# An output product by seven, a new order of the period, and tables for the opening and the closing of a two-layer graph kernel

## The chip, the cores and the metric

The kernel runs on 1 core of one Trainium2 chip. The metric is the device time of one execution in microseconds (us), lower is better. Before the change three runs gave a median of 3567.93 us (3567.24 to 3570.02).

## The reference

64 graphs of 256 nodes with 512 features, all in fp32, and for each graph an adjacency mask. Two layers follow each other, each with a layer norm and a ReLU ahead of it and a residual behind it. Cut to what matters:

```
h = maximum(layernorm(x), 0)                        # layer 0
m = h @ map_w.T + map_b                             # 512 -> 512, 8 heads of 64
cos = normalized(m) @ normalized(m).T  per head;  cos_adj = cos > 0.1
p = softmax(q @ k.T / 8, masked) * keep;  q, k = m @ q_w.T, m @ k_w.T
sem = (h @ gcn_map_w.T + gcn_map_b);  a = cos_adj * p
x = x + relu((a @ sem) @ gcn_W.T / (a.sum(-1) + 1))
h = maximum(layernorm(x), 0)                        # layer 1
q, k, v = h @ Wq, h @ Wk, h @ Wv                    # 512 -> 256, 4 heads of 64
out = softmax(masked(q @ k.T / 8)) @ v
x = x + out @ Wo + bo                               # 256 -> 512, the "output product"
```

## The kernel before, in words

All of the work is in fast_path (L153 to L1073 of the file); a general path behind a check at the end is not taken with this data. The graphs go through a software pipeline. A **period** `i` (L734) holds the steps of five graphs in different stages: the attention of layer 0 of graph `i` (`g`), the projections of layer 0 of graph `i+1` (`nx`), the norm and transposition of graph `i+2` (`n2`), the norm, projections and attention of layer 1 of graph `i-1` (`b`), and the output product and store of graph `i-2` (`bb`). A step is a function of a few instructions under a short name; the list ORDER (L716) says in which order a period calls them, and since the kernel is written with a manual schedule, that is the order of the instructions on every engine. An engine works through its own instructions strictly in that order and waits on semaphores for what comes from elsewhere. SyncE (SP) issues nearly all transfers, also in order.

The names that matter below:
- `sc0` to `sc3`: scores of layer 0 (L474, 64 rows of the array); `ex`: their exp on ScalarE (ACT); `mk`: mask on VectorE (DVE); `hv`: the two halves of a row summed on GpSimd (POOL); `co`: cosines (L511, 64 rows); `fo`, `fb`: the threshold on DVE; `fa`, `fz`: more halves on POOL; `av`: values (L501, 64 columns); `sm`, `pn`, `zb`: sums (32 columns).
- `m`, `s`, `q`, `k`, `j`, `v` with 1 to 7 and a to g: products in the manner of Strassen and Winograd (class Seven, L296). A product of 2x2 blocks takes seven block products (steps 1 to 7 on TensorE, PE) into two PSUM regions u and z, and steps a to g bring them out: a, b, c and g on ACT or DVE with the bias, d, e, f as sums on DVE (L341). Step 4 writes where step 3 wrote, so it waits for b; 5 waits for d, 6 for e, 7 for f. The sums of blocks of the weights are made once by finish_seven (L82), four DVE subtractions, and those of the data per graph by left_factor (L277), four POOL operations (`lm`, `lh`, `lb`).
- `po0`, `po1` (product_out, L697): the output product of layer 1, for each half of the nodes two matmuls of 512 columns; `oa` (added, L703) adds it to x on DVE, `st` stores.
- `rt`, `rc`, `rk`: the sums are transposed on PE, inverted on DVE, and multiplied by keep on DVE; `ho`, `ha`: the heads are scaled and added to x on DVE; `nb`: statistics of layer 1's norm on DVE; `pb`: its power on POOL; `xb`, `fl`, `tr`, `jb`: scaling, splitting into 16-bit halves, transposing by DMA, joining; `un`: the unit vectors for the cosines, on DVE; `dv` (L694): the attention of layer 1 times its inverse sums, on DVE.

PSUM is a ring of 8 banks with which all products are served. SBUF buffers of one use share a tag; the tags "xn" (2 buffers) and "d" (6), "rn" (1) and "sms" (1) matter here.

Opening (L1001 to L1068): loads, 14 warming matmuls, then the layer 0 projections of graph 0 in straight order, with finish_seven in blocks of four subtractions between the products; then 63 periods, ORDER with those steps that have a graph; then closing (L878), which runs the attention of graph 63, layer 1 of graph 62 and then layer 1 of graph 63 in straight order. The chain of layer 1's norm in it (moments, powers, scaled, split, turn, join1) has nothing of another graph beside it.

Of the kernel before, what the change touches and what calls it, by code (L numbers as in the profile page):

```python
# [20 lines left out]
LN_EPS = 1e-5  # L21
# [8 lines left out]
class Weights:  # L30
# [30 lines left out]
    def load_w(self, key, name):  # L61
        ap = self.a[key]
        t = self.const.tile([128, ap.shape[0] // 128, ap.shape[1]], F32, name=name)
        self.nc.sync.dma_start(out=t, in_=ap.rearrange("(c p) f -> p c f", p=128))
        return t

# [15 lines left out]
    def finish_seven(self, t):  # L82
        sub = self.nc.vector.tensor_sub
        sub(t[:, 5], t[:, 2], t[:, 3])
        sub(t[:, 3], t[:, 3], t[:, 0])
        sub(t[:, 4], t[:, 2], t[:, 3])
        sub(t[:, 6], t[:, 1], t[:, 4])
# [14 lines left out]
    def load_rest(self):  # L102
        self.wv1 = self.load_seven("Wv", "wv1")
        self.wqk1 = self.load_seven(("Wq", "Wk"), "wqk1")
        self.wo1 = self.load_w("Wo", "wo1")
# [17 lines left out]
    def fold(self, gws, gt, bank, put, cs):  # L123

        nc, P = self.nc, 128
        NKC = self.gb.shape[1]
        for c in cs:
            p = bank(f"p_wc{c}", [P, NKC * P])
            for k in range(NKC):
                nc.tensor.matmul(p[:, k * P:(k + 1) * P], gws[k // 2][:, k % 2, c * P:(c + 1) * P], gt,  # L130
                                 start=True, stop=True)
            put(c, p)
# [4 lines left out]
    def fold_bias(self, gbb, gt, bank):  # L137
# [5 lines left out]
        nc.scalar.copy(self.bc, p)  # L143

    def put_seven(self, c, p):
        i, k = divmod(c, self.wc.shape[2])
        half = self.wc.shape[3]
        for j in range(2):
            self.nc.scalar.copy(self.wc[:, self.BLOCKS.index((i, j)), k, :], p[:, j * half:(j + 1) * half])


@with_exitstack
def fast_path(ctx, tc, a, w, chk, out):  # L153
# [28 lines left out]
    class Graph:  # L182
        pass

    graphs = {}

    def load(i):
        g = graphs.setdefault(i, Graph())
        g.i, g.e, g.d, g.far = i, {}, {}, {}
# [4 lines left out]
        return g  # L194


    def moments(g, tag):
        st = small.tile([P, NT, 6], F32, tag="st", name=f"st{tag}", bufs=2)
        g.mv = small.tile([P, NT, 2], F32, tag="mv", name=f"mv{tag}")
        for t in range(NT):  # L200
            nc.vector.bn_stats(st[:, t, :], g.xs[:, t, :])  # L201
            nc.vector.bn_aggr(g.mv[:, t, :], st[:, t, :])  # L202
        g.rs = small.tile([P, NT], F32, tag="rs", name=f"rs{tag}")
        nc.vector.tensor_scalar_add(g.rs, g.mv[:, :, 1], LN_EPS)
# [4 lines left out]
    def normalized(g, tag):  # L209
        g.xn = []  # L210
        for t in range(NT):
# [1166 lines left out]
```

## Time and profile before

| what | us |
|---|---|
| median of 3 runs | 3567.93 |
| the profiled execution | 3568.4 |
| its span on the core | 3566.6 |
| PE busy | 3523.6 |
| DVE, ACT, POOL busy | 2285.5, 2224.8, 2499.7 |
| one period (rt of one to rt of the next) | 54.55 |
| PE busy in the first 89.00 us, in the last 97.00 us | 73.20, 69.97 |

The page gives busy time for each engine, then the span in 40 slices of 89 us (a digit is the busy share in tenths), then the chain of work that ended last. A line of a group or of the timeline has the line of the code, the engine, the operation, and `out<-in` by tile names; PEld is the weight load, which runs beside the matmuls. On PE each fp32 matmul of the program shows as two records. Durations of matmuls overlap, so what one costs is read from one start to the next. In the timeline a bracket at the end of a line is the idle time ahead of it and what ended it.

### The profile page before, as it was taken

The page shows a single profiled execution, that of the slowest core. Times are in us where ns is not written, and L with a number is a line of the kernel's source. Part 1 is how long each engine was busy: PE and PEld are TensorE (multiplying, and loading weights), DVE is VectorE, ACT ScalarE, POOL GpSimd, SP SyncE. Part 2 cuts the span into 40 slices and gives each one's busy share as a digit, 9 for nine tenths or more (in the row PEclk, how much of TensorE's full clock was granted, in tenths as well). Part 3 has the DMA queues.
Part 4 walks back from the last instruction along what each step waited for, and adds up shares of the span by engine and source line. Part 5 has one row for each costly group of instructions (what it writes and reads, how often), then busy time and mean ns, then how long its engine had stood idle before and what let it go on. Part 6 is the DMA issues. An engine that isn't in the chain of part 4 may idle for free.

```text
span 3566.6 us, 77423 instructions
## 1 busy us (share of the span) xinstructions
PE 3523.6 (99%) x28983; PEld 2996.0 (84%) x28983; DVE 2285.5 (64%) x4718; ACT 2224.8 (62%) x5302; POOL 2499.7 (70%) x2612
## 2 busy tenths in 40 slices
PE   8999999999999999999999999999999999999997
PEld 7888888888888888888888888888888888888885
DVE  5666666656667666666566666666666766666654
ACT  3666666666666666666666666666666666666652
POOL 4777777677677777776776777777767777777662
PEclk9999999999999999999999999999999999999998
DMA  4333333323333333333333333333333333333321
GB/s 115 73 67 71 83 68 71 76 66 78 69 72 80 67 71 83 67 71 75 68 77 69 72 81 67 71 79 68 73 73 71 77 68 71 82 68 71 76 55 37
DMA packets 650851, 258.32 MB, mean 72 GB/s; under 512 B 562508, under 2 KB 616808, under 8 KB 650472
## 3 DMA queue, kind: packets, MB, share of 16 engines
q1 hardware_dynamic: 649736, 252.75, 31.8%
q8 instruction: 231, 3.78, 0.5%
q14 instruction: 148, 1.21, 0.1%
q10 hardware_dynamic: 544, 0.52, 0.0%
q0 software_dynamic: 192, 0.04, 0.0%
HBM read 94.41 MB, written 34.34 MB: 36 GB/s over the span
## 4 chain that ended last, share of the span: by engine, by line
PE 97%; DMA 1%; DVE 1%; ACT 1%; POOL 0%; issue 0%; SPq 0%; DVEq 0%; POOLq 0%; ACTq 0%
PE av L501 10%; PE p_m_z L316 7%; PE p_q_z L316 7%; PE sc L474 7%; PE p_qk_z L316 6%; PE p_k_z L316 6%; PE p_o L700 6%; PE p_s_z L311 6%; PE co L511 5%; PE p_s_u L311 5%; PE p_qk_u L316 5%; PE p_k_u L316 5%; PE p_q_u L316 5%; PE p_m_u L316 5%; PE sd L474 3%; PE p_v_z L311 3%
## 5 line engine op out<-in xcount | busy, mean ns | idle before, releaser
L542 POOL TENSOR_TENSOR d<-d,e 128x512 f32<-128x512 f32 x504 | 652.9, 1316 | 158.1 <-DVE e L547 136.4
L494 POOL TENSOR_TENSOR d<-e 128x512 f32<-128x512 f32 x376 | 470.7, 1273 | 345.6 <-DVE e L488 176.7
L481 ACT ACTIVATE e<-sc 128x512 f32<-128x512 f32 x520 | 268.3, 603 | 143.8 <-PE sc L474 143.8
L488 DVE SCALAR_TENSOR_TENSOR e<-mask,e 128x1024 f32<-128x1024 bf16 x128 | 157.6, 1232 | 300.5 <-ACT e L481 237.8
L490 DVE TENSOR_TENSOR e<-e,mask 128x1024 f32<-128x1024 f32 x256 | 307.4, 1221 | 2.7 <-ACT e L481 0.4
L527 DVE SCALAR_TENSOR_TENSOR e<-co,e 128x256 f32<-128x256 f32 (+1 forms) x1024 | 286.8, 346 | 19.8 <-ACT up L520 17.8
L251 POOL COPY flat<-xn 128x512 uint16<-128x512 uint16 x252 | 218.5, 906 | 86.9 <-ACT xn L243 86.9
L474 PE MATMUL sc<-qT,kT 64*128 64x256 f32 x2048 | 238.4, 383 | 0.5 <-ACT qT L334 0.5
L501 PE MATMUL av<-e,sem 128*64 128x256 f32 x2048 | 235.4, 382 | 2.1 <-DVE e L547 2.1
L334 ACT ACTIVATE u3p_m<-p_m_u,bm 128x128 f32<-128x128 f32 x128 | 40.0, 363 | 307.8 <-PE p_m_u L316 307.8
L700 PE MATMUL p_o<-wo,own 128*128 128x512 f32 x512 | 230.6, 593 | 0.0
L474 PEld LDWEIGHTS sc<-qT,kT 64*128 64x128 f32 x2048 | 192.8, 187 | 41.4 <-issue 20.9
L229 POOL TENSOR_SCALAR shift<-mv 128x2 f32<-128x2 f32 x125 | 27.8, 222 | 282.3 <-DVE mv L202 282.3
L501 PEld LDWEIGHTS av<-e,sem 128*64 128x64 f32 x2048 | 141.4, 137 | 93.0 <-ACT v L328 25.5
L201 DVE BATCH_NORM_STATS2 st<-xs 128x6 f32<-128x512 f32 x256 | 173.3, 677 | 50.5 <-DMA xs<-in_x_dram 47.0
L243 ACT ACTIVATE xn<-xs,shift,rs 128x512 f32<-128x512 f32 x250 | 197.8, 824 | 8.5 <-POOL shift L233 8.5
L511 PE MATMUL co<-nT 64*128 64x256 f32 (+1 forms) x2048 | 202.8, 337 | 0.0
L481 ACT ACTIVATE e<-sd 128x512 f32<-128x512 f32 x248 | 134.7, 595 | 106.7 <-PE av L501 78.1
L511 PEld LDWEIGHTS co<-nT 64*128 64x128 f32 x2048 | 166.9, 187 | 40.6 <-ACT up L520 20.9
L341 DVE TENSOR_TENSOR qT<-p_q_z,u2p_q 128x256 f32<-128x256 f32 x64 | 27.1, 424 | 255.0 <-PE p_q_z L316 255.0
L442 POOL TENSOR_TENSOR lengths<-lengths,root 128x16 f32<-128x16 f32 x64 | 186.4, 2912 | 3.8 <-DMA lengths<-rn 3.8
L576 ACT COPY sem<-heads 128x512 uint16<-128x512 uint16 x252 | 178.4, 777 | 6.4 <-DMA heads<-avs 5.9
(254 smaller groups left out, 9858.0 us busy)
## 6 DMA issues: line engine op xcount, KB each, us to landing
xs<-in_x_dram SPq DMA_DIRECT2D x64, 512.0 KB, 4.1
nT<-by_rn SPq DMA_DIRECT2D x128, 256.0 KB
out_dram<-xs SPq DMA_DIRECT2D x63, 512.0 KB, 3.1
own<-by_rz SPq DMA_DIRECT2D x126, 128.0 KB, 3.1
turn<-flat SPq DMA_TRANSPOSE x500, 2.5
ad<-in_adj_dram SPq DMA_DIRECT2D x64, 64.0 KB
far<-up SPq DMA_TRANSPOSE x256, 3.1
heads<-avs SPq DMA_TRANSPOSE x252, 2.5
```

The costliest lines, as they stand in the source:

```text
L251: copy(getattr(g, what)[:, t, k, :], g.xn[t].bitcast(U16).rearrange("p (d k) -> p k d", k=2)[:, k, :])
L311: nc.tensor.matmul(region, src[:, c, :], self.wt[:, block, c, :], start=p not in self.opened, stop=True, skip_group_check=True)
L316: nc.tensor.matmul(region[:, f, :], self.wt[:, block, c, f * P:(f + 1) * P], src[:, c, :], start=p not in self.opened, stop=True, skip_gro ...
L474: nc.tensor.matmul(ps[s][:, j, :], rows[h, c, j * P:(j + 1) * P], cols[h, c, :], start=True, stop=True)
L481: nc.scalar.activation(e[:, s, :], p.rearrange("p j q -> p (j q)"), AF.Exp, scale=SCALE)
L490: nc.vector.tensor_mul(e, e, m)
L494: nc.gpsimd.tensor_add(d, e[:, :, :S], e[:, :, S:])
L501: nc.tensor.matmul(av[s * DH:(s + 1) * DH, n, :], vs[:, j, (h0 + s) * DH:(h0 + s + 1) * DH], q[:, s, j * S:(j + 1) * S], start=(j == 0), s ...
L511: nc.tensor.matmul(ps[s][:, j, j * P:], g.nT[h, c, j * P:(j + 1) * P], g.nT[h, c, j * P:], start=(j == 0), stop=True, skip_group_check=True)
L527: nc.vector.scalar_tensor_tensor(e, p.rearrange("p j q -> p (j q)")[:, lo:hi], THRESHOLD, e, op0=ALU.is_gt, op1=ALU.mult)
L542: nc.gpsimd.tensor_add(g.d[c][:, :, q], g.d[c][:, :, q], g.e[c][:, :, lo:hi])
L700: nc.tensor.matmul(p, b.avs1[:, c, t * P:(t + 1) * P], w.wo1[:, c, :], start=(c == 0), stop=(c == NIC - 1))
```

## The change

Three things. First, the output product is one of the sevens: Wo is loaded in four blocks, its block sums are made in the opening (`fw0` to `fw3`), its data's block sums are four POOL steps `lw0` to `lw3`, written where the inverse sums `z` lay, and the steps are `w1` to `w7` and `wa` to `wg` with x in the place of a bias, on DVE (`onto`). Each product is one matmul of 256 columns. For the last graph by_halves does the same with five matmuls per half of the nodes and no block sums of the data. Second, ORDER is new; it serves periods 2 to 61. Third, periods 0 and 1 with all of the opening are one table (HEAD), and periods 62, 63 and 64 with all of the closing are another (TAIL); finish_seven is cut into single steps. Layer 1 of graph 62 then takes the steps of the period (`hy`, `zb` on halves). Besides: "xn" and "d" become one tag "xd" with 7 buffers, "rn" and "sms" one tag "row" with 1, and graph 3 is loaded early in HEAD rather than after period 0.

```diff
-        self.wo1 = self.load_w("Wo", "wo1")
+        self.wo1 = self.load_seven("Wo", "wo1")
...
-    def finish_seven(self, t):
...
+    def finish_one(self, t, n):
+        to, x, y = ((5, 2, 3), (3, 3, 0), (4, 2, 3), (6, 1, 4))[n]
+        self.nc.vector.tensor_sub(t[:, to], t[:, x], t[:, y])
...
+def by_halves(nc, p, rows, wt):
+
+    half = wt.shape[3]
+    for f, terms in enumerate((((0, 0), (1, 1)), ((0, 3), (0, 0), (1, 2)))):
+        for n, (c, block) in enumerate(terms):
+            nc.tensor.matmul(p[:, f * half:(f + 1) * half], rows(c), wt[:, block, 0, :],
+                             start=(n == 0 and f == 0), stop=(n == len(terms) - 1), skip_group_check=True)
...
-            setattr(g, f"left_{kind}", sb1.tile([P, 4, HC, P], F32, tag=tag, name=f"{tag}_{kind}{g.i}"))
+            setattr(g, f"left_{kind}", g.z.rearrange("p c (n q) -> p (c n) q", q=P)[:, :, None, :] if kind == "avs1"
+                    else sb1.tile([P, 4, HC, P], F32, tag=tag, name=f"{tag}_{kind}{g.i}"))
...
-            for c in range(HC):
+            for c in range(self.wt.shape[2]):
...
-        def biased(self, t, region, features):
-            if self.bias is None:
+        def biased(self, t, region, tokens, features):
+            if self.onto:
+                nc.vector.tensor_add(t, region, self.quarter(tokens, features))
+            elif self.bias is None:
...
-    def product_out(b, t):
-        p = bank(f"p_o{b.i}_{t}", [P, D])
-        for c in range(NIC):
-            nc.tensor.matmul(p, b.avs1[:, c, t * P:(t + 1) * P], w.wo1[:, c, :], start=(c == 0), stop=(c == NIC - 1))
-        return p
...
+    def outputs(b):
+        return Seven((b, "avs1"), w.wo1, None, lambda: b.xs, f"p_o{b.i}", tokens_first=True, onto=True)
 
-    ORDER = """
-        s2 s1 sc2 rk sc0 sc1 ho0 ho1 ha0 ha1 mt nb ex2 ex0 mk2 sc3
-        s3 sb m1 ex3 dv ex1 mk3 sa m2 sd m3 po0 po1 s5 pb xb0
-        xb1 ma un oa0 md mb fl01 mk1 m5 m4 mc co0 up0 co1 fl00 fl10
-        mk0 fl11 hv0 hv1 up1 oa1 tr00 tr01 tr10 jb0 st tr11 ft0 rq s4 me
-        fo0 sc ft1 se ld co3 co2 m6 s6 fo1 mf m7 k1 rr jb1 hv3
-        hv2 fa1 v1 mg fo2 fa0 fo3 lm0 up2 na lm1 ft2 lb0 lb1 lb3 pa
-        lm3 j2 j1 q1 j3 k3 q3 up3 va ja sf jd jb fb1 lb2 j4
-        jc fb0 j5 je xa0 v2 pl00 ft3 v3 vb xa1 vd k2 j6 pl10 v5
-        v4 jf qa fa2 fb2 fa3 fz2 fz1 bo1 ka pl11 kd vc ve fb3 kb
-        pl01 ta00 s7 j7 v6 ta01 ta10 k4 vf v7 kc jg sq0 sq1 k5 sd0
-        sg fz3 sd1 pn ey0 my0 fz0 hy0 ln av0 vg ey1 ja0 hs00 my1 av1
-        hy1 hs10 ay sm zb ls bo0 hs01 qb q2 ta11 ht00 ht01 ht10 ke to
-        hs11 hj00 ht11 qd iy ed q4 qc lm2 q5 qe rt k6 q6 kf li
-        ja1 lh2 lh0 lh1 lh3 k7 sy sp qf rc hj01 hj10 hj11 q7 zq kg
-        qg oy
-    """.split()
+    ORDER = """
+        sc3 rk ho0 sc0 ex3 sc1 ex1 ha0 rq ho1 ha1 dv lw0 sc2 w1 w3
+        w2 s1 lw1 lw3 nb wa wd ex2 s2 wb w4 w5 m1 mk2 pb xb0
+        lw2 xb1 fl00 fl11 fl01 ex0 wc we m2 w6 m3 sa un ma mb wf
+        sd w7 wg rr s3 md sb mk1 co2 co3 up3 up2 s4 hv2 mk3 mk0
+        fo2 fl10 m4 tr00 mc tr01 s5 tr10 st tr11 m5 sc se co0 co1 s6
+        jb0 hv3 hv0 hv1 ft2 me up0 m6 fo0 jb1 j1 fo3 mf fa0 lb2 lb0
+        lb1 v1 m7 lb3 up1 ld sf mg j2 v2 j3 v3 s7 lm0 na pa
+        vb ja mt xa0 jd fo1 ft0 fb0 va fa2 fa1 fz0 lm1 fa3 fb2 pl00
+        q1 fz2 pl01 ft1 ta01 ft3 fb1 fz1 bo1 q3 j5 v4 jb xa1 vc pl11
+        vd j4 jc je q2 v5 ve qa j6 jf v6 k1 ta00 ka vf sg
+        v7 pl10 ta11 ta10 j7 k3 jg lm3 bo0 sq1 sq0 qb vg sd1 sd0 fb3
+        ey0 av0 av1 ey1 ja0 q4 hs00 k2 hs01 kb k4 ja1 qd my0 my1 kc
+        pn hs10 ln hy0 hy1 zb fz3 lm2 sm lh2 ay ht00 ht01 ls hj00 hs11
+        lh0 lh1 ht10 hj01 qc kd hj10 iy q5 qe k5 ke ht11 lh3 to sy
+        q6 qf hj11 k6 li sp rt kf rc q7 qg oy ed k7 kg zq
+    """.split()
...
-            each(T, "po%d")(lambda t: bb.po.update({t: product_out(bb, t)}))
-            each(T, "oa%d")(lambda t: added(bb, t, bb.po[t]))
+            left("lw", bb, "avs1")
+            seven("w", outputs(bb))
...
+    HEAD = """
+        o.na00 o.na01 o.nr0 o.w0 o.ed0 o.dn0 o.xn00 o.tp00 o.tq00 o.xn01 o.tp01 o.tq01 o.lh00 o.lh01 o.lh03 o.fm0
+        o.fm1 o.l3 o.fm2 o.fm3 o.lh02 o.ed1 o.gb o.fp2 o.m1 o.fp0 o.m3 o.fp3 o.ma o.m2 o.mb o.fo2
+        o.m4 o.fq0 o.md o.fk0 o.mc o.m5 o.me o.fp1 o.m6 o.fo3 1.na o.mt0 o.mf o.q2 o.q1 o.m7
+        o.fk1 o.fo0 o.k1 o.fk2 o.sq1 o.fq1 o.fo1 o.mg o.sq0 o.na10 o.na11 o.nr1 o.ka o.lm0 o.bp o.pn
+        o.s1 o.q3 o.lm1 o.k2 o.bo o.lm2 o.qa o.fs0 o.fq2 o.ln 0.na o.fs1 o.qd o.lm3 o.k3 o.qb
+        o.s2 o.q4 o.q5 o.kb o.dn1 o.qc o.sa 0.pa o.fs2 o.qe o.xn10 o.sd 0.mt 0.xa0 0.pl01 0.xa1
+        o.s3 o.q6 o.k4 o.kc o.kd o.qf o.sb o.xn11 o.k5 o.fk3 o.s4 o.s5 o.ke o.sc o.se o.k6
+        o.s6 0.pl00 o.ls o.fw0 o.fw1 o.kf 0.sc2 0.ex2 o.k7 o.fs3 o.sf o.fj0 o.fq3 0.mk2 o.s7 o.tp10
...
+        1.co2 1.mk1 1.lw0 1.w3 1.tr11 1.ft3 1.up2 1.ft2 1.up0 1.ft0 1.mk3 1.w2 c.se1 c.se3 1.wb 1.fo2
+        1.lw1 1.wd 1.fo3 1.fb3 1.co1 1.jb0 1.jb1 1.up1 1.lw3 1.w4 1.bo1 1.lb0 1.w5 1.j1 1.ft1 1.j3
+        1.rq 1.fb2 1.fb0 1.lb1 1.lb3 1.lw2 1.fo1 1.fb1 1.wc 1.we 1.av1 1.av0 c.sm0 c.sm2 c.sm1 c.vs0
+        1.jb c.vs1 c.fi c.sm3 c.to c.hb0 c.hb1 1.rt 1.rc 1.w6 1.wf 1.j2 1.ja c.rk c.hm0 c.hp0
+        1.w7 1.jd 1.j4 1.lb2 1.j5 1.v2 1.v1 1.jc 1.je 1.j6 c.hm1 1.va 1.vd c.hp1 1.jf c.nb0
+        c.nb1 1.v3 1.vb 1.j7 1.v5 1.v4 1.jg c.nr c.dn 1.vc 1.sd0 1.ve 1.ey0 1.sd1 1.v6 c.xn0
+        c.xn1 c.tp1 c.tp0 1.ey1 c.tq0 1.vf 1.my0 1.my1 1.v7 1.vg 1.ay c.tq1 0.j1 0.ja 1.hy0 1.hy1
+        0.lb0 1.zb 0.v2 0.j3 0.j2 0.lb1 c.rq 1.zq 1.iy 0.lb3 0.lb2 1.wg 0.jb 0.jd 0.j4 0.j5
+        0.v1 0.v3 0.jc 0.je 1.oy 0.vb 0.va 0.rr 0.j6 0.v4 0.vc 0.vd 0.v5 0.jf 0.j7 0.ve
+        1.sy 0.dv 0.jg 0.v6 0.sd0 0.vf 0.sd1 1.bo0 0.w1 0.lw0 0.lw1 0.bo1 0.w3 0.ey0 0.my0 0.w2
+        2.st 1.st 0.lw3 0.lw2 0.bo0 0.ey1 0.my1 0.v7 0.vg 0.wb 0.wa 0.wd c.zl 0.ay 0.w5 c.zi0
+        c.zm0 c.zi1 0.w4 c.zm1 c.zk c.po0 0.wc 0.we 0.w6 0.wf c.po1 c.oa0 c.oa1 0.w7 c.wu 0.wg
+        c.st0 c.st1 0.st
+    """.split()
...
-        for i in range(B - 1):
-            period(i)
-        closing()
+        tables = {"o": opening_steps()}
+        heads, tails = {0: 0, 1: 1}, {2: B - 2, 1: B - 1, 0: B}
+        for n, i in heads.items():
+            tables[f"{n}"] = steps_of(i)
+        for name in HEAD:
+            table, name = name.split(".")
+            tables[table][name]()
+        for i in range(2, B - 2):
+            steps = steps_of(i)
+            for name in ORDER:
+                steps[name]()
+        tables = {"c": closing_steps()}
+        for n, i in tails.items():
+            tables[f"{n}"] = steps_of(i)
+        for name in TAIL:
+            table, name = name.split(".")
+            tables[table][name]()
```

opening_steps and closing_steps (new) hold the former steps of the opening and the closing under names of their own ("o." and "c." in the tables), cut smaller: for example `o.tp00` the four transposes of one half of the nodes, `c.zi0` the reciprocal of one half. steps_of is the former period, without the loop over ORDER.

## The prediction

> **What bounds the kernel now.** I read the page first (busy shares, slices, chain), then the stretches, then the PE timeline of one period in the middle and of both ends.
>
> ```profile
> span 3566.6 us, 77423 instructions
> ...
> PE 3523.6 (99%) x28983; PEld 2996.0 (84%) x28983; DVE 2285.5 (64%) x4718; ACT 2224.8 (62%) x5302; POOL 2499.7 (70%) x2612
> ...
> PE   8999999999999999999999999999999999999997
> ...
> PE 97%; DMA 1%; DVE 1%; ACT 1%; POOL 0%; issue 0%; SPq 0%; DVEq 0%; POOLq 0%; ACTq 0%
> ```
>
> TensorE is the bound: 97% of the chain, and only the first and the last slice are not full. So every us must come out of three things: PE's own work, waits in the first and last 90 us, and waits that a new order may put into the middle. The stretches say the same:
>
> ```profile
> 0.00:89.00 89.00, 73.20 (x544) 63.97 (x548) 50.95 (x111) 33.04 (x84) 44.27 (x53) 0.98 0.42 115
> ...
> 1780.00:1834.50 54.50, 54.50 (x452) 46.40 (x451) 35.26 (x73) 35.05 (x84) 39.28 (x42) 1.00 0.32 74
> ...
> 3470.00:3567.00 97.00, 69.97 (x543) 52.77 (x543) 46.18 (x90) 31.93 (x81) 21.14 (x23) 0.90 0.14 39
> ```
>
> Columns: stretch, length, busy us of PE, weight load, DVE, ACT, POOL, then granted clock. The middle one is a period (54.55 us from one rt product, 1781.64, to the next, 1836.19): PE busy throughout, the others with 15 to 19 us to spare.
>
> The price of PE work comes from the timeline (start, duration, what):
>
> ```profile
> 1786.29 1.03 PE L311 MATMUL p_s_u<-wc,hT 128*128 128x256 f32 x4
> 1787.25 3.72 PE L474 MATMUL sc<-qT,kT 64*128 64x256 f32 x32
> ...
> 1794.55 3.60 PE L700 MATMUL p_o<-wo,own 128*128 128x512 f32 x8
> 1797.99 1.03 PE L311 MATMUL p_s_z<-wc,sh_hT 128*128 128x256 f32 x4
> 1798.85 1.05 PE L316 MATMUL p_m_z<-sh_hT,wm 128*128 128x128 f32 x8
> ...
> 3498.77 2.08 PE L316 MATMUL p_qk_u<-h1T,wqk 128*128 128x128 f32 x8 [14.29 <-ACT h1T L267]
> ```
>
> Durations overlap, so the cost is start to start. Each fp32 matmul of the program is two records. Eight records 512 wide take 1797.99 - 1794.55 = 3.44 us (0.430 each); four 256 wide take 0.86 (0.215 each). A change of tile shape costs extra: the four of p_s_u ahead of the 64-row sc take 0.96. Over all neighbouring pairs that extra is 0.093 us, and nothing else in the middle exceeds the bare price: no idle over 0.06 us between 110 and 3476 us. The last line is the end's largest wait, 14.29 us, with the restart at half clock (2.08 against 1.06).
>
> **The change part by part**, against the profiled execution (3568.4 us; span 3566.6).
>
> *Output product by seven.* Before: 8 records of 0.430 per graph, 3.44 us. Now seven block products of one 256-wide matmul each: 14 records of 0.215, the price of the row with the same form (p_s_z), 3.01 us. Gain 0.43 for 63 graphs; the last graph's (by_halves) takes 10 matmuls for 8 equivalents, 0.86 more. 63 x 0.43 - 0.86 = -26.2 us; at the mean intervals of all pairs (0.429, 0.216) it is -24.8, which I take. The weight load of each (0.19 us) stays under the matmul, as in p_s.
>
> *More changes of tile shape.* The new ORDER puts q4, k2, k4 between the value products (av0, av1) and pn: one more change per period; the two end tables add the rest. Counting along PE's instruction order of both programs: 709 before, 784 after. The Trainium skill speaks against this: TensorEngine Tiling (Array Packing), Key Properties, says that changing the mode drains the engine. It gives no figure there; TensorE: Matmul & The Clock Gate, Step-by-step, puts a drain at about 128 cycles, 53 ns at 2.4 GHz. By that, 75 x 0.053 = 4.0 us; by the trace's 0.093, 7.0 us. The trace is taken: +7.0.
>
> *DVE and POOL work of the product.* DVE adds five more operations of 128x256 (7 against 2 of 128x512): 7 x 0.42 - 2 x 0.69 = +1.6 us per period on 35.3. POOL adds four lw sums of 128x128; no row has that size: 0.73 us (128x256) is the upper bound, half of it the lower; I take 0.45, as 128x512 costs 1.27 and 128x256 0.73. +1.8 on 39.3. Both stay far below 54, so in total they cost nothing; what matters is where they stand.
>
> *New waits at the period's start.* This is the unknown term. PE now comes from rt through q7, k7 and four sc to w1: 0.22 + 1.79 + 3.65 + 0.09 = about 5.76 us after rt starts. w1 needs dv. On DVE, in order ahead of dv: kf, rc, rk, ho0, ha0, ho1, ha1. Their rows:
>
> ```profile
> 1784.18 0.25 DVE L608 RECIPROCAL r<-rt 128x16 f32<-128x16 f32 x1
> 1784.47 0.86 DVE L618 TENSOR_SCALAR rk<-r,keep 128x8 f32<-128x8 f32 x2
> 1785.30 1.96 DVE L630 SCALAR_TENSOR_TENSOR o<-sem,rk 128x256 f32<-128x256 f32 x4
> 1787.18 1.28 DVE L636 TENSOR_TENSOR xs<-xs,o 128x512 f32<-128x512 f32 x2
> 1788.49 0.69 DVE L201 BATCH_NORM_STATS2 st<-xs 128x6 f32<-128x512 f32 x1
> ...
> 1790.44 1.23 DVE L490 TENSOR_TENSOR e<-e,mask 128x1024 f32<-128x1024 f32 x1
> ```
>
> k6 ends when rt starts; its result is there 0.2 later. Then kf 0.38, rc 0.29, rk 0.83, ho 1.88, ha 1.31, dv 0.65: dv ends 5.5 to 5.6, against 5.76. Just in time. w3, 0.43 after w1, needs dv and then lw0 (0.45 plus two handovers): late by up to 0.1. DVE goes on without a gap: nb 1.95, wa, wd, wb 1.1 (w4 waits for wb: on time to 0.1 late), mk2 1.2, wc, we, sa 1.2, un 1.4, wf 0.4. That ends 12.9 after rt; w7, which waits for wf, is due at 12.8. Behind w1, w3, w4, w7 stands all of PE's queue (s1, m1, m3, s3, co), so such a lateness is paid in full, once per period, as the chain hangs on rt again. Below nothing is excluded: PE had no idle there to give back. From above: 0.4 us, if each handover costs 0.05 more. I take 0.1, close to the sum: 60 x 0.1 = +6 us, and keep 0 and 24. Elsewhere I find cover of 0.2 us or more (s6 waits for se, j1 for jb1, sm for the last fz). On SP the output store now waits for wg, before the last turn; wg ends about 1 us before SP gets there (fl10 comes later on POOL). The shared buffers cost nothing in the middle: sms waits until the lengths' transfer has read its row, about 1.5 us earlier.
>
> *Opening.* PE idles 16.3 us up to 115 us (brackets of the PE timeline, summed), 2.8 of it before anything can run:
>
> ```profile
> 21.61 2.08 PE L316 MATMUL p_m_z<-sh_hT,wm 128*128 128x128 f32 x8 [3.15 <-DVE mT L341]
> ...
> 39.52 1.16 PE L316 MATMUL p_q_z<-sm_mT,wq 128*128 128x128 f32 x8 [2.67 <-DVE qT L341]
> ...
> 81.47 1.13 PE L316 MATMUL p_k_u<-sm_mT,wk 128*128 128x128 f32 x8 [3.41 <-ACT u5p_k L334]
> ```
>
> The 3.15 stands behind the four subtractions for wq on DVE; in the table they come later and one by one, and fold, q, k or s products stand between an m product and its successor. The start itself (statistics, pow, transposes, first product at about 10 us) is unchanged. I leave 5 us: -11.3, between -6 and -13.5. PE also ran at half clock from 21.6 to 25.0 after that wait: -1.7.
>
> *Closing.* PE idles 19.9 us from 3470 on, of which 14.3 in one wait (moments, pow, copies, turns and joins of graph 62 with nothing beside them). In the table periods 62 and 63 and the closing interleave, so that chain lies under other products. What remains is the last graph's own chain (values, sums, norm, transposes, scores, exp, reciprocals), with graph 62's j, v and w as fillers: I leave 7, so -12.9 (between -7 and -17), and -2.2 for the half clock after 3498.8. On the other side the last store is now 512 KB issued after wg, where it was 256 KB: its row lands in 3.1 us against 1.7: +2. The kernel's last 5.4 us (the check and what follows) stay.
>
> Sum: -24.8 + 7.0 + 6 - 11.3 - 1.7 - 12.9 - 2.2 + 2 = -37.9; 3568.4 - 37.9 = 3530.5. The median of the runs is 0.5 under the profiled one: 3530.
>
> **The rivals.**
> 1. *The new order's waits take the middle's gain.* At 0.5 us per period: 24 us more, 3554. For it: DVE has no gap for 12 us there, and four PE waits hang on it. Against: the sum ends within 0.1 us. Chance 0.17.
> 2. *Nothing waits.* The middle fits, and both ends keep only what no order can remove (about 3 us at each): -6 - 2 - 4 - 2 = 3516. For it: the old order has no wait in the middle either. Chance 0.13.
> 3. *Slower: DVE and POOL collide at the period's start.* The Trainium skill, SBUF — State Buffer, Who interferes with whom, says that a DVE instruction with two SBUF inputs and a GpSimd instruction that reads SBUF exclude each other for a whole instruction. The trace has such spread: the far products (L547, two SBUF inputs) take 0.41 to 0.97 us for one shape, the pow (L207) 0.73 to 1.76. The change puts lw0, lw1, lw3, lw2 beside dv, mk2, un, all with two SBUF inputs. By the rows alone the chain is 0.1 late; if each of three pairs blocks for 0.4 to 0.5 us, it is 1.4 late: 60 x 1.3 = 78 more, 3608. It decides from 0.85 us per period: slower by 0.2% is 3575, 45 us over the forecast, so 0.75 per period beyond the 0.1 already in it. Against: the rows of ho, ha and mk were taken with POOL working beside them. Chance 0.05.
> My forecast, 3516 to 3543 with its bounds: 0.62. Something small of everything that leaves about 3563 to 3573: 0.03.
>
> **How the numbers follow.** 3530. The range, 3511 to 3555, takes the forecast, most of rival 2 and rival 1 up to its middle; 0.2 stays outside. A measurement of this kernel tells about 0.2% (7 us) from no change: faster means under 3560.8. Forecast, rival 2 and nearly all of rival 1 lie there: 0.92; same 0.03; slower 0.05.
>
> **What would show it.** The product: p_o rows of 256 at 0.215 start to start, 3.0 us per graph. The period from rt to rt: 54.24 without waits (54.55 - 0.41 + 0.09), 54.3 to 54.4 by my forecast, over 54.7 by rival 1, over 55.4 by rival 3, with the idle ahead of p_o_u, p_o_z and released by DVE or POOL. PE idle up to 115 us near 5, in the last 100 us near 7, and no half clock in between. It would be wrong if PE shows idle at other places of every period (se before s6, jb1 before j1), if the last chain is longer than its fillers by more than 7 us, or if the weight load comes out from under a 256-wide matmul.

## The result and the profile after

The changed kernel takes 3544.51 us (median of 4 runs, 3544.05 to 3544.79) against 3568.78 us for the kernel before in the same session (3567.24 to 3570.02). The ratio is 0.9933 with a 95% interval of 0.9917 to 0.9948. So it is faster by 24 us, where the forecast was 38.

The page of the profile after, the same lines as before (span, busy time, PE's slices, the chain's shares):

```profile
span 3543.0 us, 78756 instructions
...
PE 3518.9 (99%) x29365; PEld 3090.2 (87%) x29365; DVE 2340.2 (66%) x5037; ACT 2227.0 (63%) x5302; POOL 2694.2 (76%) x2866
...
PE   8999999999999999999999999999999999999999
...
PE 97%; DMA 1%; DVE 1%; ACT 0%; SPq 0%; issue 0%; POOL 0%; DVEq 0%
```

The last slice is full now, the first is not: it is still an 8. The stretches say by how much (length, busy us of PE, weight load, DVE, ACT, POOL, then granted clock):

```profile
0.00:89.00 89.00, 74.12 (x558) 66.88 (x559) 52.45 (x117) 37.46 (x91) 46.34 (x57) 0.92 0.45 122
1776.70:1831.15 54.45, 54.45 (x458) 47.94 (x458) 37.14 (x78) 35.06 (x84) 41.13 (x46) 1.00 0.31 73
3446.00:3543.00 97.00, 88.90 (x715) 68.87 (x711) 56.26 (x112) 39.87 (x104) 44.60 (x43) 0.99 0.18 49
```

PE's busy time in the last 97 us rose from 69.97 to 88.90 us. In the first 89 us it rose by 0.9 only, and the clock fell from 0.98 to 0.92. Cut at the rt products (start of the first rt of a graph on PE), the difference of the two spans, -23.6 us, falls apart like this:

| part | forecast | measured |
|---|---|---|
| opening, up to rt of graph 2 (199.59 before, 198.78 after) | -13.0 | -0.8 |
| 59 periods, to rt of graph 61 (3418.16 before, 3411.98 after) | -12.7 | -5.4 |
| from there to the end | -12.2 | -17.4 |

(The forecast's middle row is 59 x -0.215, from a period of 54.55 before to 54.335; its last row is what remains of -37.9. One of the 59 measured periods takes 55.49 us and costs 1.0 of the middle once.) The opening gave nothing, the middle less than half, the closing more than was asked of it.

**The opening.** PE of the changed kernel:

```profile
22.59 1.06 PE L316 MATMUL p_q_z<-mT,wq 128*128 128x128 f32 x8
23.48 1.06 PE L316 MATMUL p_q_u<-mT,wq 128*128 128x128 f32 x8
33.61 2.08 PE L316 MATMUL p_m_z<-hT,wm 128*128 128x128 f32 x8 [9.08 <-DVE mT L343]
35.48 1.91 PE L316 MATMUL p_k_u<-mT,wk 128*128 128x128 f32 x8
```

A single stand of 9.08 us, and the work after it at half clock: eight records take 1.87 us from start to start (33.61 to 35.48) where they take 0.89 (22.59 to 23.48). The bracket names DVE's mT, step mf. So the next view is DVE's timeline, and behind its bracket SP's (issues of transfers):

```profile
21.05 0.42 DVE L343 TENSOR_TENSOR mT<-p_m_z,u3p_m 128x256 f32<-128x256 f32 x1 [0.77 <-PE p_m_z L316]
31.32 0.69 DVE L198 BATCH_NORM_STATS2 st<-xs 128x6 f32<-128x512 f32 x1 [9.85 <-DMA xs<-in_x_dram]
...
33.14 0.42 DVE L343 TENSOR_TENSOR mT<-p_m_z,u5p_m 128x256 f32<-128x256 f32 x1
```

```profile
22.89 2.30 SPq L73 DMA_DIRECT2D wo<-in_L_gnn_Wo_dram  x3
...
26.31 0.38 SPq L190 DMA_DIRECT2D xs<-in_x_dram  x1
```

DVE stands for 9.85 us at a bn_stats (L198). That is 1.na in HEAD, the statistics of graph 3, and it stands two places ahead of mf. Its input is issued by SP at 26.31 us, behind all weights, and is there only at 31.3. A second stand lies underneath, on POOL:

```profile
32.38 0.62 POOL L381 TENSOR_SCALAR home<-ad 128x512 bf16<-128x512 uint8 x1 [17.93 <-DMA mask<-home]
...
36.44 0.73 POOL L288 TENSOR_TENSOR sm_mT<-mT 128x256 f32<-128x256 f32 x1 [3.16 <-ACT mT L336]
```

o.ed1 (L381, edges of graph 1) waits 17.93 us for the DMA transposes of graph 0's mask, which read the one buffer it writes, and lm0 (sm_mT, L288) is next behind it.

**The middle.** The period is 54.44 us. The product does as predicted (PE, start to start):

```profile
1780.77 3.73 PE L468 MATMUL sc<-qT,kT 64*128 64x256 f32 x32
1784.42 1.13 PE L311 MATMUL p_o_u<-wo,own 128*128 128x256 f32 x4
1785.39 0.59 PE L311 MATMUL p_o_z<-wo,own 128*128 128x256 f32 x2
1785.82 1.03 PE L311 MATMUL p_s_u<-wc,hT 128*128 128x256 f32 x4
```

Two records of p_o take 0.43 us (1785.39 to 1785.82). No line here has a bracket: w1, w3, w2 begin on time. But the first line, w1 and w3 in one group, takes 0.97 us for four records, not 0.86. It is the first product in the full array after the 64-row sc. The same 0.10 us more stands behind every return to the full array, in the kernel before too (p_s_u takes 1.13 us behind sc there and 1.03 elsewhere in the period). I counted changes of shape by what the work ahead of the change takes longer, and this I missed. Now to the new stay (q4, k2 and k4 at the full array between two smaller shapes). What it costs is read from both periods, from sd to the next q product. Before:

```profile
1769.60 2.00 PE L474 MATMUL sd<-qk 64*128 64x256 f32 x16
1771.52 0.64 PE L421 MATMUL p_n<-sq,blk 128*32 128x256 f32 x8
1772.09 3.67 PE L501 MATMUL av<-e,sem 128*64 128x256 f32 x32
...
1778.31 0.61 PE L678 MATMUL zb<-d,ones 128*32 128x256 f32 x8
1778.86 1.16 PE L316 MATMUL p_q_z<-mT,wq 128*128 128x128 f32 x8
```

After:

```profile
1817.26 2.00 PE L468 MATMUL sd<-qk 64*128 64x256 f32 x16
1819.19 3.67 PE L495 MATMUL av<-e,sem 128*64 128x256 f32 x32
1822.80 1.16 PE L316 MATMUL p_q_u<-sm_mT,wq 128*128 128x128 f32 x8
1823.79 1.06 PE L316 MATMUL p_k_z<-mT,wk 128*128 128x128 f32 x8
1824.68 1.08 PE L316 MATMUL p_k_u<-sm_mT,wk 128*128 128x128 f32 x8
1825.70 0.64 PE L415 MATMUL p_n<-sq,blk 128*32 128x256 f32 x8
...
1829.44 1.16 PE L316 MATMUL p_q_z<-sm_mT,wq 128*128 128x128 f32 x8
```

Before: 1778.86 - 1769.60 = 9.26 us. After: 12.18 less three q and k products of 0.895, 9.50. The difference is 0.24 us, of which 0.03 is a small wait at p_k_u; so a stay costs 0.21, not 0.093. The rest of the surplus is waits, and none of them where I looked. The largest, PE and then DVE:

```profile
1812.18 0.68 PE L311 MATMUL p_v_z<-wv,sh_h1T 128*128 128x128 f32 x4
1812.70 1.06 PE L316 MATMUL p_qk_z<-sh_h1T,wqk 128*128 128x128 f32 x8
```

```profile
1808.63 3.27 DVE L536 SCALAR_TENSOR_TENSOR e<-far,e 128x256 f32<-128x256 bf16 x3
1811.82 0.28 DVE L343 TENSOR_TENSOR v<-p_v_z,u2p_v 128x128 f32<-128x128 f32 x1
```

POOL beside it:

```profile
1808.60 1.27 POOL L531 TENSOR_TENSOR d<-d,e 128x512 f32<-128x512 f32 x1 [0.62 <-DVE e L521]
1810.23 1.38 POOL L531 TENSOR_TENSOR d<-d,e 128x512 f32<-128x512 f32 x1 [0.36 <-DVE e L536]
```

p_v_z takes 0.52 in place of 0.45 us: v5 waits 0.07 us in every period for vd (L343), which stands behind three far products (fb, L536) on DVE. These three take 1.52, 0.41 and 1.49 us one by one. The first and the third begin 0.03 and 0.18 us after one of the two POOL sums and end 0.28 us after it; the second begins while POOL idles. Sum for a period: 54.55 - 0.43 (product) + 0.21 (stay) + 0.03 + 0.07 + 0.02 (a like wait at q6) = 54.45.

**The closing.** PE idles 2.1 us from 3470 us on, where it was 19.9; the largest stand is 0.45 us:

```profile
3524.96 1.08 PE L898 MATMUL z<-e,ones 128*64 128x256 f32 x8 [0.30 <-DVE e L482]
3531.44 0.67 PE L311 MATMUL p_o_z<-wo,own 128*128 128x256 f32 x2 [0.45 <-DVE xs L343]
...
3534.53 2.17 PE L997 MATMUL warm<-ident 128*128 128x128 f32 x18
```

The last line counts as busy but makes no result: nine warming matmuls (`c.wu` in TAIL). In the kernel before they stood ahead of the last graph's layer 1 products (at 3530.78, 36 us ahead of the end); here they stand behind the last product, with only the small p_ok after them, and the chain that ended last runs through them for 2.0 us. p_ok starts at 3536.81; in the kernel before it came 0.15 us behind the last addition on DVE, which here ends at 3535.32. By these times up to 1.3 us could be won without them, an estimate that no run tried.

### The profile page after: what moved, and what is told of

Same layout as the page of the kernel before. It is cut to its first block, busy times and chain, and to the rows that moved or that the text cites. A ratio compares the mean times of both kernels' runs of the same rounds, so it can differ in the third digit from the quotient of the medians.

```text
span 3543.0 us, 78756 instructions
## 1 busy us (share of the span) xinstructions
PE 3518.9 (99%) x29365; PEld 3090.2 (87%) x29365; DVE 2340.2 (66%) x5037; ACT 2227.0 (63%) x5302; POOL 2694.2 (76%) x2866
## 4 chain that ended last, share of the span: by engine, by line
PE 97%; DMA 1%; DVE 1%; ACT 0%; SPq 0%; issue 0%; POOL 0%; DVEq 0%
PE av L495 10%; PE p_q_z L316 7%; PE sc L468 7%; PE p_s_z L311 7%; PE p_k_z L316 6%; PE p_qk_z L316 6%; PE p_m_z L316 6%; PE co L505 5%; PE p_q_u L316 5%; PE p_s_u L311 5%; PE p_k_u L316 5%; PE p_qk_u L316 5%; PE p_m_u L316 5%; PE sd L468 3%; PE p_v_z L311 3%; PE p_o_z L311 3%
## 5 line engine op out<-in xcount | busy, mean ns | idle before, releaser
L488 POOL TENSOR_TENSOR d<-e 128x512 f32<-128x512 f32 x378 | 641.7, 1717 | 365.4 <-DVE e L484 220.3
L475 ACT ACTIVATE e<-sc 128x512 f32<-128x512 f32 x512 | 275.7, 593 | 46.0 <-PE sc L468 45.9
L565 ACT COPY sem<-heads 128x512 uint16<-128x512 uint16 x252 | 196.7, 783 | 121.1 <-DMA heads<-avs 121.1
L514 ACT ACTIVATE up<-co,below 128x128 bf16<-128x128 f32 x512 | 153.3, 369 | 131.1 <-PE co L505 131.0
L536 DVE SCALAR_TENSOR_TENSOR e<-far,e 128x256 f32<-128x256 bf16 x256 | 232.6, 947 | 0.8 <-DMA far<-up 0.8
L253 POOL COPY flat<-xn 128x512 uint16<-128x512 uint16 x252 | 201.9, 827 | 35.1 <-ACT xn L245 35.0
L288 POOL TENSOR_TENSOR own<-own 128x128 f32<-128x128 f32 x63 | 28.6, 455 | 248.2 <-DVE own L667 248.2
L495 PEld LDWEIGHTS av<-e,sem 128*64 128x64 f32 x2048 | 141.4, 137 | 85.4 <-issue 19.9
L198 DVE BATCH_NORM_STATS2 st<-xs 128x6 f32<-128x512 f32 x256 | 172.4, 673 | 13.6 <-DMA xs<-in_x_dram 13.3
L265 ACT COPY hT<-turn 128x1024 uint16<-128x1024 uint16 x124 | 172.8, 1394 | 0.3 <-issue 0.3
L269 ACT COPY h1T<-turn 128x1024 uint16<-128x1024 uint16 x126 | 170.9, 1359 | 1.3 <-DMA turn<-flat 1.3
```

What stands on the lines that cost most here:

```text
L253: copy(getattr(g, what)[:, t, k, :], g.xn[t].bitcast(U16).rearrange("p (d k) -> p k d", k=2)[:, k, :])
L475: nc.scalar.activation(e[:, s, :], p.rearrange("p j q -> p (j q)"), AF.Exp, scale=SCALE)
L488: nc.gpsimd.tensor_add(d, e[:, :, :S], e[:, :, S:])
L495: nc.tensor.matmul(av[s * DH:(s + 1) * DH, n, :], vs[:, j, (h0 + s) * DH:(h0 + s + 1) * DH], q[:, s, j * S:(j + 1) * S], start=(j == 0), s ...
L536: nc.vector.scalar_tensor_tensor(e, g.far[c], 0.0, e, op0=ALU.is_gt, op1=ALU.mult)
```

## The experiments

The changed kernel was timed in the first session only, and the kernel before had medians from 3568.8 to 3570.5 us in the four sessions of these runs. Differences of 1 to 2 us between them are therefore read from the start of graph 2's rt in the traces, not from the medians.

The theory after this reading: the opening lost its gain to two orders in the table, each of which puts an in-order engine in front of a late transfer; the middle lost 0.1 us a period to the price of a stay and 0.1 to small waits. The rivals: the opening is bound by the arrival of its loads, and any wait taken away is replaced by another; and the product's own additions on DVE and POOL cost what the middle lacks.

**x3_early**: graph 3's input is issued ahead of the last weights.

```diff
+        xs3 = graphs[3]
+        xs3.xs = io.tile([P, NT, D], F32, tag="xs", name="xs3")
+        nc.sync.dma_start(out=xs3.xs, in_=x_t[3])
         w.load_rest()
```

> The order of all steps as in the changed kernel, but the transfer of graph 3's x is issued ahead of the layer 1 weights instead of behind them. Theory (it is the landing of that transfer that DVE waits for): it lands about 10 us sooner, near 21 us, the DVE wait shrinks to under 1 us and the time falls by 10 to 14 us, as in the run that moves the step. Rival (the position of the statistics is what hurts, by DVE work): 1.9 us of DVE work stays there, so no more than 2 us less.

Measured: 3538.67 us, ratio 0.9917 (0.9904 to 0.9931). The stand before p_m_z fell from 9.08 to 3.61 us, DVE's at the statistics from 9.85 to 4.38. The time fell by 5.8 us, which is neither the theory's 10 to 14 nor the rival's 2 at most. The transfer is the cause of the stand, but even when issued earlier it lands late.

**na_late**: the statistics are called on DVE only just ahead of their use.

```diff
-        ... o.m6 o.fo3 1.na o.mt0 ...
+        ... o.m6 o.fo3 o.mt0 ...
-        ... o.tq11 1.pa ...
+        ... o.tq11 1.na 1.pa ...
```

> One step moved in the opening's table: the statistics of graph 3 (1.na, on DVE) stand just ahead of their use (1.pa) instead of in the middle of graph 0's first product. Theory (DVE, in order, stood 9.85 us behind the transfer of graph 3's x, and with it the sum mf that PE's m7 needs): the PE wait of 9.08 us at 24.5 us goes, and with it the half clock from 29.6 to 39.8 us, which cost about 5 us of PE time: 10 to 14 us less, about 3532 us. Rival (the wait only moves to the next late thing, the chain from squares to lengths to spread): 0 to 4 us less.

Measured: 3541.86 us, ratio 0.9925 (0.9912 to 0.9939). The stand before p_m_z is gone, and 2.6 us are won. PE and POOL show where the rest went:

```profile
34.12 2.07 PE L316 MATMUL p_q_u<-sm_mT,wq 128*128 128x128 f32 x8 [6.70 <-POOL sm_mT L288]
```

```profile
32.52 0.62 POOL L381 TENSOR_SCALAR home<-ad 128x512 bf16<-128x512 uint8 x1 [18.11 <-DMA mask<-home]
...
33.35 0.72 POOL L288 TENSOR_TENSOR sm_mT<-mT 128x256 f32<-128x256 f32 x1
```

PE now stands 6.70 us for lm0, which comes right behind o.ed1 on POOL. So far the rival (a wait only moves) has the better of it; the theory in its first form, one wait, falls.

**na_ed_late**: o.ed1 goes behind o.lm3 besides.

```diff
-        ... o.fm3 o.lh02 o.ed1 o.gb ...
+        ... o.fm3 o.lh02 o.gb ...
-        ... o.qd o.lm3 o.k3 ...
+        ... o.qd o.lm3 o.ed1 o.k3 ...
```

> na_late with one further move in the opening's table: o.ed1 (graph 1's edges on POOL, whose one buffer is held by the transposes of graph 0's mask) goes from ahead of o.gb to behind o.lm3. In na_late PE stood 6.70 us at 27.42 us for sm_mT (o.lm0), which stood on POOL behind o.ed1. Theory (two in-order engines each stood for one late transfer, one hidden behind the other): with both moved, PE's idle time in the first 60 us falls from 14.9 in the changed kernel to 5 to 6 us, the clock is not halved for 7 to 10 us any more, and the time is 3533 us (3530 to 3536). Rival (the opening is bounded by the arrival of the weights, so that each removed wait is replaced by the next one): idle stays at 9 us or more and the time at 3539 to 3542.

Measured: 3532.68 us (3532.06 to 3534.06), ratio 0.9897 (0.9882 to 0.9913). Idle up to 60 us is 5.6 us, and the first stretch has 83.37 us of PE work at full clock:

```profile
0.00:89.00 89.00, 83.37 (x654) 76.04 (x654) 62.62 (x141) 44.95 (x110) 53.36 (x64) 1.00 0.49 133
```

The rt of graph 2 comes at 186.68, 12.9 us ahead of the kernel before. The rival is out: no further wait of that size took the place. The transposes that o.ed1 waits for still land late (POOL stands 3.65 us for them, until 32.17), but no stand of PE over 0.5 us follows.

**ed_late**: that last edit alone.

> The changed kernel with o.ed1 alone moved behind o.lm3 in the opening's table; the statistics 1.na stay where DVE stands at them for graph 3's input. Theory (two waits one behind the other, of which the earlier hides the later): alone this removes nothing, PE still stands some 9 us at 24.5 us for mT, and the time is 3544 us (3541 to 3546), though both moves together gave 3532.7. Rival (the wait on POOL was the one that mattered, and moving it is enough): 3533 to 3536.

Measured: 3543.73 us, ratio 0.9925 (0.9911 to 0.9938); PE stands 10.45 us before p_m_z. So by the medians one edit gives 2.6 us, the other 0.8 (hardly more than its runs scatter), both 11.8. The rt of graph 2 says the same within one trace each: 198.78 in the changed kernel, 195.62 in na_late, 197.87 here, 186.68 with both. These are two stands one under the other, and each covers the other.

**x3_ed**: o.ed1 late, with graph 3's input issued early in place of na_late's edit.

> The changed kernel with graph 3's input transferred ahead of the last weights, 1.na in its place, and o.ed1 moved behind o.lm3. Theory (DVE's stand at 1.na ends when its transfer lands, and that is the rest of the loss): as in x3_early the stand before p_m_z remains at 3 to 4 us since that transfer still lands behind other loads, and the second wait goes: 3536 us (3533 to 3539), slower than with 1.na moved. Rival (only the place in the queue of transfers counts, the order on DVE does not): 3530 to 3533.

Measured: 3536.57 us, ratio 0.9903 (0.9888 to 0.9918), with a stand of 3.46 us at p_m_z. Keeping the statistics out of the way is worth more than fetching their input sooner.

**wide_product**: the changed kernel with the former product, as two halves of 512 columns at the places of w1 and w4.

```diff
+            def half_out(t):
+                bb.po[t] = bank(f"p_o{bb.i}_{t}", [P, D])
+                for c in range(NIC):
+                    nc.tensor.matmul(bb.po[t], bb.avs1[:, c, t * P:(t + 1) * P], w.wo1[:, c, :], start=(c == 0), stop=(c == NIC - 1))
+            step("w1")(lambda: half_out(0))
+            step("w4")(lambda: half_out(1))
...
```

> The changed kernel with the output product taken back to two times four matmuls of 512 columns (first half at the place of w1, second at that of w4; its two additions at the places of wd and wf; the steps lw and the other w steps empty), all else as in the changed kernel. Theory (product by seven is worth 0.39 us a period and its additions and left factors hide): 3569 us (3567 to 3572), period 54.83 us. Rival (the additions on DVE and the four left factors on POOL cost waits of their own, so that less comes back): 3555 to 3564.

Measured: 3565.87 us, ratio 0.9989 (0.9982 to 0.9996). Its period is 54.85, 0.41 over the changed kernel's: in the middle the product is worth its whole price, and its additions and left factors are hidden. Over 59 periods that is 23.1 us on the rt marks. The total moved 21.4, between the two forecasts, because the end, from rt of graph 62, is 2.4 us shorter with the wide product (76.4 against 78.8). 0.9 of that is by_halves (20 records of 0.216 for 8 of 0.429), and 0.8 is idle time of PE (2.2 us in that stretch against 1.4); the cause of the rest stays open. That the idle time comes from the chain of seven (each d, e, f between two products) in a stretch with few fillers is likely, as in the 0.45 above before p_o_z, but not shown.

**seven_alone**: the kernel before with the product by seven, in its own order.

```diff
-        s3 sb m1 ex3 dv ex1 mk3 sa m2 sd m3 po0 po1 s5 pb xb0
-        xb1 ma un oa0 md mb fl01 mk1 m5 m4 mc co0 up0 co1 fl00 fl10
-        mk0 fl11 hv0 hv1 up1 oa1 tr00 tr01 tr10 jb0 st tr11 ft0 rq s4 me
+        m1 ex3 dv ex1 mk3 sa m2 sd m3 w1 w2 wa wd pb lw0 lw1 lw3 w3 s3 lw2 xb0
+        xb1 wb un ma md sb w4 w5 s5 wc we m5 w6 wf mb fl01 mk1 m4 mc co0 up0 co1 fl00 fl10
+        mk0 fl11 hv0 hv1 up1 tr00 tr01 tr10 jb0 tr11 ft0 w7 wg st rq s4 me
```

> The kernel before with the output product by seven alone: its opening, closing and its order of a period stay, save that s3 and the steps of the product are set among the full-array products m1 to m5 and s5, with w7 beside s4, so that no tile shape changes more often. Two last graphs use the product by halves. To make room in SBUF the bias of the folded weights is added in the place of bo (the same instructions), and the table of checked sums is shared by eight graphs each. Theory (the product is worth 24.8 us by itself, waits aside): 3544 us if the added steps of DVE and POOL hide, up to 3556 with 0.2 us of waits a period. Rival (it needs the new order of the period to pay): 3562 or more.

Measured: 3774.98 us, ratio 1.0571 (1.0557 to 1.0586), the period 57.67. PE, ACT and DVE:

```profile
1786.85 1.16 PE L324 MATMUL p_m_u<-sh_hT,wm 128*128 128x128 f32 x8 [1.18 <-ACT u5p_m L344]
```

```profile
1786.17 0.63 ACT L344 ACTIVATE u5p_m<-p_m_u,bm 128x128 f32<-128x128 f32 x2 [5.09 <-DVE xs L351]
```

```profile
1785.71 0.42 DVE L351 TENSOR_TENSOR xs<-p_o_z,u5p_o 128x256 f32<-128x256 f32 x1 [0.85 <-PE p_o_z L319]
```

m's kept piece (u5, ACT) waits for the output product's to be given back (wf), since the tag u5 has two buffers and s holds the other. That wait is 1.2 of the 3.5 us lost per period (3.1 over the kernel before, and the 0.43 not gained); the rest is smaller waits among the same three products and the co behind them. The edit also takes one of the two buffers of the norm's statistics (`st`), which was not tried by itself. The run shows that the product does not pay at these places of the former order; it says nothing on whether better places near it exist, so the rival is not shown.

**three_stays**: k2 goes between sd1 and sd0, one stay at the full array more.

> In ORDER alone: k2 is put between sd1 and sd0, so that the scores of layer 1 are split by one more stay in the full array. Theory (two changes at 0.093 and one slow return at 0.10): period 54.445 + 0.29 = 54.73 us, 60 x 0.29 = 17 us more, 3562 us. With changes at 0.093 alone: 54.63, 11 us more. If changes cost nothing and waits are the cause: 54.45.

Measured: 3612.73 us, ratio 1.0123 (1.0107 to 1.0138), the period 1.15 us longer. PE:

```profile
1795.27 1.13 PE L468 MATMUL sd<-qk 64*128 64x256 f32 x8
1796.33 1.16 PE L316 MATMUL p_k_z<-mT,wk 128*128 128x128 f32 x8
1797.42 1.13 PE L468 MATMUL sd<-qk 64*128 64x256 f32 x8
1799.23 3.67 PE L495 MATMUL av<-e,sem 128*64 128x256 f32 x32 [0.68 <-ACT e L475]
```

k2 takes 1.09 us start to start between two shapes and 0.895 among its like, 0.19 more. But the two halves of sd pay too: each takes 1.06 us without its wait, where the undivided pair takes 1.93: 0.20 more. Half of this is at the start of the second sd, where the first two records of 64 rows behind the full array take 0.32 us and later pairs 0.22. So this stay costs 0.39 us, not the expected 0.29. The other 0.75 of the 1.15 is a wait that the edit brought with it: the last record of sd stands for 1.06 us in place of 0.31 until the exp of the second sd lets av start (0.68 by the bracket).

**one_stay**: the opposite, pn ahead of av and q4, k2, k4 behind zb.

```diff
-        ey0 av0 av1 ey1 ja0 q4 hs00 k2 hs01 kb k4 ja1 qd my0 my1 kc
-        pn hs10 ln hy0 hy1 zb fz3 lm2 sm lh2 ay ht00 ht01 ls hj00 hs11
+        ey0 pn av0 av1 ey1 ja0 hs00 hs01 kb ja1 qd my0 my1 ln
+        hs10 hy0 hy1 ay fz3 sm zb q4 lm2 k2 k4 kc lh2 ht00 ht01 ls hj00 hs11
```

> In ORDER alone: q4, k2, k4 go behind the sums, so that scores, pn, values and sums stand together as in the kernel before (one change of tile shape and one return to the full array less per period). Theory (a stay outside the full array costs 0.093 per change and another 0.10 on the first matmuls after the return): period 54.25 instead of 54.445 us, 60 x 0.19 = 11.6 us less, 3533 us, if nothing new waits. Rival (the 0.2 us over my sum are waits for engines): period 54.4 or more. What may spoil it: ay needs the second mask my1, which would then come 0.3 to 0.7 us late; that would show as PE idle ahead of av.

Measured: 3702.93 us, ratio 1.0374 (1.036 to 1.0388). The edit brought waits: q6 stands 1.72 us; its bracket names a POOL step long done, and by the order of the work it waits for qe on DVE, qe for qc on ACT, and qc stands there behind kc and three copies. It decides nothing on the stay.

**one_stay2**: the same with qc ahead of k2 and fz3 ahead of hy0.

> one_stay again, with what stood late in it moved: qc directly behind q4 on ACT, fz3 ahead of hy0 and hy1 on POOL; so a period has one stay fewer at the full array. Theory (a stay costs 0.093 us into the shape and 0.10 us back, 0.19 us a period): 3533 us (3531 to 3537) when no wait is left. Rival (the place of pn, av and the sums is tied to ACT and POOL, so that what is saved in shapes is waited for): period 55 us or more, time over 3570.

Measured: 3562.10 us, ratio 0.9976 (0.9968 to 0.9985). Most of its periods take 54.50 us, 0.05 over the changed kernel's, and ten of them 0.6 to 2.1 us more, with sc waiting for qT or kT. Where the 0.21 went in the quiet periods is to be read on PE and ACT:

```profile
1773.20 0.64 PE L415 MATMUL p_n<-sq,blk 128*32 128x256 f32 x8
1773.95 3.67 PE L495 MATMUL av<-e,sem 128*64 128x256 f32 x32
```

```profile
1773.30 2.06 ACT L475 ACTIVATE e<-sd 128x512 f32<-128x512 f32 x4 [0.72 <-PE sd L468]
```

From p_n to av are 0.75 us, and 0.57 in the kernel before (1771.52 to 1772.09 above): 0.18 lost with no bracket. But the first of the four exps of sd ends at 1773.90, and in all 58 periods from the rt of graph 3 on, here and in one_stay, av starts 0.052 to 0.054 us after the end of that exp; in the changed kernel it starts 0.70 ahead of it. So av waits for this exp. The ring of PSUM banks fits: with pn ahead of av, q holds two banks, k one, the scores four and pn one, all eight, and the exp frees the first; that the bank is the reason was not tested. The rest of the block, from sd to the next q product, takes 8.69 in both (9.44 - 0.75 here, 9.26 - 0.57 before). So the stay's price came out and a wait of nearly the same size came in; another 0.07 is at a p_q_z. The rival has the kind right (what is saved in shapes is waited for), but not the size: 3562 us lies between the two forecasts.

**na_ed_vd**: na_ed_late with vd ahead of the far products on DVE.

```diff
-        q1 fz2 pl01 ft1 ta01 ft3 fb1 fz1 bo1 q3 j5 v4 jb xa1 vc pl11
-        vd j4 jc je ...
+        q1 fz2 pl01 ft1 ta01 ft3 vd fb1 fz1 bo1 q3 j5 v4 jb xa1 vc pl11
+        j4 jc je ...
```

> na_ed_late, and in the period's order vd moved from behind vc and pl11 to ahead of fb1, so that it doesn't stand on DVE behind three far products (3.27 us); v5 waited 0.071 us a period for it. Theory: 59 periods lose 0.07 us each, 3528.5 us (3527 to 3530), period 54.37 us. Rival (the far products come 0.35 us later, and what waits for them takes the place): 3532 to 3534, period 54.44 or more.

Measured: 3529.64 us (3528.57 to 3530.59), ratio 0.9884 (0.9868 to 0.9899), the period 54.37. It is the fastest of all, 14.9 us under the changed kernel, by three names in two tables. Beside na_ed_late the 59 periods gained 4.2 us on the rt marks; in its profiled run the opening stood longer (8.4 us idle up to 60 us against 5.6), so the two profiled executions differ by 1.5 only, the medians by 3.0. Part of that is the wait seen before: o.ed1 starts at 34.06 in place of 32.17, because the transposes of the mask landed later, and PE loses 1.48 us at a p_k_z behind it. Issuing them ahead of the last weights was not tried.

## Why the prediction was right or wrong

- *The product*: right. Forecast 0.41 to 0.43 us a period, 0.43 in the trace and 0.41 by wide_product; its work on DVE and POOL is hidden, as said.
- *The opening*: wrong, and the step that failed is "I leave 5 us: -11.3", with the 1.7 for the half clock. Idle up to 60 us alone is 14.9. I went through the waits of the kernel before and said that the table fills them. I did not go through what the table moves ahead: graph 3's statistics, which before came in period 1, now stand on DVE ahead of mf, and its transfer is last in SP's queue behind every weight; o.ed1 on POOL stands ahead of lm0. With those two moved the opening ends 12.9 us earlier than before, against 13.0 forecast. So the size was right for a table without these two places, and the runs show that they were the whole loss (12.2 of it missing, 12.1 returned by na_ed_late). That 12.9 meets 13.0 so closely is chance: with the same table of the opening, na_ed_vd's trace ends it 2.5 us later.
- *The half clock*: it had to go and grew instead. A stand of 9.08 us was followed by 6.2 us of work at half clock (33.6 to 39.8), some 3 us lost. This was a consequence of the same step.
- *Changes of shape*: mis-sized. The term of 0.093 us counts the work ahead of the change; the first product back in the full array costs 0.10 more. The new stay is 0.21 us by the two periods: 59 x 0.117 = 6.9 us too little. Between two pieces of 64-row work it is 0.39 (three_stays). The rule that the Trainium skill states on this (TensorEngine Tiling (Array Packing), Key Properties: a change of mode drains the engine) points the right way; the 53 ns that the prediction took for a drain would have been further off.
- *Waits at the period's start*: forecast 0.1 us at w1, w3, w4 or w7, measured none there. But the sum behind it was off by a microsecond to the safe side. After the rt of a graph, dv ends at 4.6 us and not at 5.5 to 5.6, with w1 due at 5.75:

```profile
1778.67 0.38 PE L593 MATMUL rt<-ident,sms 128*128 128x128 f32 x2
```

```profile
1782.57 0.69 DVE L667 TENSOR_TENSOR own<-own 128x512 f32<-128x512 f32 x1
```

The rows that the sum used were stretched. In the kernel before, the first rk takes 0.73 us and the first ho 0.95, each beside a POOL sum and ending 0.03 and 0.28 us after it; here they take 0.23 and 0.42, while POOL stands idle for 4.0 us, since its next step, lw0, itself waits for dv. Waits of 0.12 us in all turned up elsewhere, at v5, k4 (p_k_u) and q6, which "elsewhere I find cover of 0.2 us or more" had passed over. The total of the term was about right by luck: its place and its margin were wrong. Rival 1 (0.5 us) is out. Rival 3 is out in its size and place; its mechanism, that DVE and POOL exclude each other, agrees with the trace (far products of 1.52 and 1.49 us where one takes 0.41 with POOL idle), and that puts vd late and makes v5 wait, at 0.07 us a period.
- *The closing*: better than forecast, -17.4 against -12.2. I left 7 us of idle for the last graph's own chain; 2.1 are left, or 4.1 with the warming matmuls on the chain, since the fillers of graphs 61 and 62 suffice. The last store's +2 is hardly to be seen: from the end of the last product to the end of the span are 8.3 us, 7.9 before.

The forecast missed by 14 us: 12 in the opening and 7 in the middle, less 5 that the closing gave over. The range of 3511 to 3555 would have held without the closing's surplus too (3544.5 + 5.2 = 3549.7). It held because it had been made wide for another cause, waits at the period's start (rival 1), which did not come; that the opening's failure fell inside it is luck.

## What to carry to other kernels

When a table moves work forward, cost what it moves, not only the hole it fills: for each step that now stands earlier, ask which transfer it needs, where that transfer is in its queue, and who stands behind the step on its in-order engine. When one wait is removed and little is won, look for a second one underneath before giving the cause up: here either edit alone gave 0.8 to 2.6 us, both together 11.8. Read the price of a shape change from the work on both of its sides. And before a row's duration goes into a sum, look at what the neighbouring engine did beside it: here the same DVE instruction took 0.23 or 0.73 us.

## What the runs showed of the hardware

- A change of tile shape is paid on both sides. The work ahead of it takes 0.09 to 0.11 us longer, into a smaller shape and back alike. The first product back in the full 128x128 array takes 0.10 us longer (1.13 or 1.16 in place of 1.03 or 1.06 in the row), after 64-row, 64-column and 32-column work alike; the first 64-row work takes 0.10 longer too (three_stays). One stay at the full array costs 0.21 us between 64-column and 32-column work (changed kernel), 0.39 between two pieces of 64-row work (three_stays).
- A DVE instruction that begins just behind a POOL sum can last until after its end: far products of 1.52 and 1.49 us against 0.41 with POOL idle (changed kernel), rk 0.73 against 0.23 (kernel before and changed kernel).
- What a stop of PE costs in clock does not simply follow its length. The granted clock stayed whole after stands of 1.4 to 1.6 us (na_ed_late, na_ed_vd). In the kernel before a stand of 3.15 us (at 21.61) brought 3.4 us of half clock, one of 3.41 us (at 81.47) none. After 3.61 us it was halved for 3.4 us (x3_early), after 6.70 for 6.8 (na_late), after 9.08 and 10.45 for 10.2 (changed kernel, ed_late). The halving begins 4.1 to 5.0 us after the start of a stand from 3.61 us up, so part of it can pass in the stand: with work were 3.4, 4.2, 6.2 and 4.4 us of it.
